# Settling keys and adding values one slot later, and pools whose tiles wait for their own bytes, in a two-layer Perceiver block on one core

## The chip, the core and the metric

The kernel runs on one core of a Trainium2 chip. The metric is the device time of one execution in microseconds. Of three runs the median is 1718.99 us (1718.89 to 1719.83). The core has five engines with a queue of instructions each: TensorE (PE in the profile; its weight loads are PEld), VectorE (DVE), ScalarE (ACT), GpSimd (POOL) and SyncE (SP, which here only issues loads and stores). They meet at semaphores.

## What is computed

x holds 512 tokens of width 512, the context 8192 rows of width 512. Two layers follow each other; a layer is three residual steps, each on a layer norm of x:

```
x = x + cross_attention(ln(x), context)   # 16 heads of 32; layer 0 also normalizes each head's q and k
x = x + self_attention(ln(x))             # layer 0: causal to later tokens; layer 1: a window of 64
x = x + experts(ln(x))                    # 8 experts, the best 2 of each token (silu / squared relu)
```

Cross attention is, per head, `softmax(q k^T masked) v`, with keys and values projected from the context. The masks leave few context rows in play (the inputs mask all but the tail), so the fast path looks for the tiles of 128 context rows that hold an unmasked row, up to 15 of them (SLOTS), and works on those alone. A path for more tiles is in the program and not run on these inputs.

## The kernel before

The order of stages is cross attention 0, self-attention 0, experts 0, cross attention 1, self-attention 1, experts 1. The framework (a tile scheduler) chooses the order of instructions on each engine when the program is built, mostly the order in which they are written, with a ready one put ahead of one that waits; it also adds the semaphores. Tiles come from pools. A pool is a stretch of SBUF (or of PSUM banks) and is opened and closed like a bracket, so that a later pool can take the memory of one that was closed. Within a pool a tag has a number of buffers, used in turn.

Cross attention (`attend_slots`) runs in two stages for each layer.

**The key stage** goes through the slots `s`. `keys(s)` projects a slot's keys into the one bank of `pacc`; in layer 0 VectorE adds the bias into a tile `kb` (L1051). `unit(s)` normalizes its heads (`unit_rows`: a square on ScalarE L1099, a sum L1101, a square root on ScalarE L172, a reciprocal L174, a product L1103). `settle(s)` transposes `kb` on TensorE (L1060, tile `ktp`) and ScalarE copies it with norm weights into `kT` (L1061). In layer 1 the keys are written into `kT` directly and `settle` and `unit` do nothing. `maxima(0, s)` makes the scores of the first of four groups of heads for that slot and takes running maxima on VectorE (`take`, L763 and L765). `values(s)` projects values (`pv`). In layer 0 `beside()` also goes through the second layer's mask: a load of 512 KB, a column on GpSimd and squares on ScalarE (L1204). The slot loop runs keys(s), settle(s-1), maxima(0, s-2), values in about half of the slots of layer 0, unit(s), beside. Ahead of it in layer 0 `queries` makes q in four token tiles with the same unit_rows; its tile `qb` shares the tag and two buffers with `kb`. Behind the loop come the last maxima, the row shifts of group 0 (`shift_of`: transposes `mtp`, then reductions) and the maxima of group 1 for four slots.

**The attention** goes through 4 groups x 15 slots. A step makes four score tiles (`sc`, four heads), subtracts the row maxima by a small matmul (L639), takes exponentials on ScalarE into a `pT` tile (L869), and adds the values of the step before (`accumulate`, tile `acc`, L824). The denominators are summed on GpSimd (VectorE in the last group) into `four` tiles (L842) and reduced by TensorE (L851); `divide` takes their reciprocal (L861). The first 41 steps also carry the maxima of a later group (`scm`), in two halves; the last 19 don't, and are called plain steps here. Work such as the outputs (`ops`, L712) is spread over later steps as fillers. PSUM has eight banks: four with tag `s`, three with `m`, one for `acc`; score tiles of plain steps take `s` and `m` in turn.

Self-attention and experts open their pools on memory that the stages before have used (`self_and_ffn`). The experts' layer norm writes `xn` (L189), transposes it (`lnt`, L192), makes router logits (`lps`, L1686), and only then knows which experts' weights to load (L1665, L1670). A branch (`tc.If`, for inputs with fuller experts) ends each expert stage and isn't taken.

Of the kernel before, what the change touches and what calls it, by code (L numbers as in the profile page):

```python
# [55 lines left out]
def tile_perceiver(  # L56
# [6 lines left out]

    const = ctx.enter_context(tc.tile_pool(name="const", bufs=1))
# [9 lines left out]
    dram = ctx.enter_context(tc.tile_pool(name="dram", bufs=1, space=bass.MemoryType.DRAM))  # L74
# [22 lines left out]
    with tc.tile_pool(name="begins", bufs=1) as tmp, tc.tile_pool(name="beginsps", bufs=1, space=PSUM) as tps:  # L97
        t = tmp.tile([1, NCHUNK, CH // P], F32, name="brow")
        nc.gpsimd.iota(
            t, pattern=[[NC * CH // P, NCHUNK], [1, CH // P]], base=0, channel_multiplier=0,  # L100
            allow_small_or_imprecise_dtypes=True,
        )
        tp = tps.tile([NKT, 1], F32, name="bcol")
        nc.tensor.transpose(tp, t.rearrange("p n i -> p (n i)"), ident[0:1, 0:1])
        nc.vector.tensor_copy(begins, tp)
# [311 lines left out]
    def cross_attention0():  # L417
        with ExitStack() as st:
            pool = st.enter_context(tc.tile_pool(name="c0", bufs=2))
            ctxp = st.enter_context(tc.tile_pool(name="ctxp0", bufs=2))  # L420
            psum = st.enter_context(tc.tile_pool(name="c0ps", bufs=2, space=PSUM))
            pacc = st.enter_context(tc.tile_pool(name="c0acc", bufs=1, space=PSUM))
# [3 lines left out]
            with tc.tile_pool(name="c0q", bufs=2) as qp:  # L426
# [8 lines left out]
            kvp = st.enter_context(tc.tile_pool(name="c0kv", bufs=NCHUNK // 2))  # L435
# [70 lines left out]
    def cross_attention1():  # L506
        with ExitStack() as st:
            pool = st.enter_context(tc.tile_pool(name="c1", bufs=2))
            ctxp = st.enter_context(tc.tile_pool(name="ctxp1", bufs=2))
            psum = st.enter_context(tc.tile_pool(name="c1ps", bufs=2, space=PSUM))  # L510
            pacc = st.enter_context(tc.tile_pool(name="c1acc", bufs=1, space=PSUM))
# [3 lines left out]
            with tc.tile_pool(name="c1q", bufs=2) as qp:  # L515
# [7 lines left out]
            kvp = st.enter_context(tc.tile_pool(name="c1kv", bufs=NCHUNK))  # L523
            mp = st.enter_context(tc.tile_pool(name="c1m", bufs=2))
# [212 lines left out]
    def attend_slots(pool, psum, pacc, kT, vN, qT, kbias, wo, bv, late, keys, settle, values, unit, more, early, aside, beside, extra):  # L737
# [47 lines left out]
        for s in range(n):  # L785
            keep(keys, s)
            if s >= 1:
                settle(s - 1)
            if s >= 2:
                maxima(0, s - 2)  # L790
# [5 lines left out]
            beside()  # L796
        settle(n - 1)
        steps = shift_of(0)
# [3 lines left out]
        keep(values, todo.pop(0))  # L802
# [11 lines left out]
        last = None  # L814

        def accumulate():

            if last is None:
                return
            g, i, pT = last  # L820
# [50 lines left out]
        for at in range(NG * n):  # L871
            g, i = divmod(at, n)
            mg, mi = divmod(at + n + LEAD, n)
            pT = late().tile([P, GH, S], F32, name="pT", tag="pT", bufs=4)
            if mg < NG:

                for j in range(2):
# [12 lines left out]
                    if j == 0:  # L890
                        accumulate()
# [3 lines left out]
            else:  # L895
# [7 lines left out]
                accumulate()  # L903
# [9 lines left out]
            last = (g, i, pT)  # L913
# [9 lines left out]
        accumulate()  # L923
        denominators(NG - 1, range(end - 2, end), end)
        for _, f in fillers:
# [30 lines left out]
    def cross_slots0():  # L956
        with ExitStack() as st:
            pool = st.enter_context(tc.tile_pool(name="f0", bufs=2))
            psum = st.enter_context(tc.tile_pool(name="f0ps", bufs=4, space=PSUM))
            pacc = st.enter_context(tc.tile_pool(name="f0acc", bufs=1, space=PSUM))  # L960
# [4 lines left out]
            kvp = kv.enter_context(tc.tile_pool(name="f0k", bufs=2))  # L965
            qp = kv.enter_context(tc.tile_pool(name="f0q", bufs=2))
# [57 lines left out]
            def queries(behind):  # L1024
                with tc.issue_after(behind.ins):
                    for t in range(NT):
# [6 lines left out]
                        qb = kvp.tile([P, D], F32, name="qb", tag="kb")  # L1033
# [13 lines left out]
            def keys(s):  # L1047
                pk = pacc.tile([P, D], F32, name="pk", tag="acc")
                half(s, 0, pk)
                kb = kvp.tile([P, D], F32, name="kb", tag="kb")  # L1050
# [32 lines left out]
            def late():  # L1083
                if not over:
                    kv.close()
                    over["pool"] = st.enter_context(tc.tile_pool(name="f0w", bufs=2))
# [18 lines left out]
    def cross_slots1(irow, kbias):  # L1105
        with ExitStack() as st:
            pool = st.enter_context(tc.tile_pool(name="f1", bufs=2))
            psum = st.enter_context(tc.tile_pool(name="f1ps", bufs=4, space=PSUM))
            pacc = st.enter_context(tc.tile_pool(name="f1acc", bufs=1, space=PSUM))
# [4 lines left out]
            kvp = kv.enter_context(tc.tile_pool(name="f1k", bufs=2))  # L1114
            qp = kv.enter_context(tc.tile_pool(name="f1q", bufs=2))
# [51 lines left out]
            def late():  # L1167
                if not over:
                    kv.close()
                    over["pool"] = st.enter_context(tc.tile_pool(name="f1w", bufs=2))  # L1170
# [87 lines left out]
    def self_attention0(pool):  # L1258
        with ExitStack() as st:
            psum = st.enter_context(tc.tile_pool(name="s0ps", bufs=3, space=PSUM))  # L1260
            pacc = st.enter_context(tc.tile_pool(name="s0acc", bufs=1, space=PSUM))
# [124 lines left out]
    def self_attention1(pool):  # L1386

        W = S + 2 * PAD
        with ExitStack() as st:
            psum = st.enter_context(tc.tile_pool(name="s1ps", bufs=3, space=PSUM))  # L1390
            pacc = st.enter_context(tc.tile_pool(name="s1acc", bufs=1, space=PSUM))
# [264 lines left out]
    def ffn(wp, pool, w1, w2, ff, layer, act, softmax_first, caps, order):  # L1656
# [20 lines left out]
        with ExitStack() as st:  # L1677
            psum = st.enter_context(tc.tile_pool(name="fps", bufs=2, space=PSUM))
            pacc = st.enter_context(tc.tile_pool(name="facc", bufs=1, space=PSUM))
            inner = st.enter_context(tc.tile_pool(name="finner", bufs=2))  # L1680
# [203 lines left out]
    def rest(wp, pool, weights, irow, place, gate, xn, n, act, caps):  # L1884

        with ExitStack() as st:
            psum = st.enter_context(tc.tile_pool(name="rps", bufs=2, space=PSUM))
            pacc = st.enter_context(tc.tile_pool(name="racc", bufs=1, space=PSUM))
# [256 lines left out]
```

## Time and profile before

| | |
|---|---|
| runs, median | 1718.99 us |
| profiled execution | 1715.68 us, its span 1713.8 us |
| mean granted TensorE clock | 0.941 |
| cross attention 0: head and key stage | 0 to 203 us |
| cross attention 0: attention, plain steps from 409 | 203 to 479 us |
| self-attention 0 | 479 to 650 us |
| experts 0 | 650 to 948 us |
| cross attention 1 (plain steps from 1299) | 954 to 1368 us |
| self-attention 1 | 1368 to 1493 us |
| experts 1 | 1493 to 1701 us |

The stretches are read from the order of instructions in time. In the page, "busy" is the time in which an engine had an instruction; a line of the slices has 40 digits, one for 42.8 us each, in tenths. A line of waits reads: the engine, tile and line that waited, the engine, tile and line that released it, then the total in us, how many times and the longest. A line of the timeline reads: start, length, engine, line, instruction, output and inputs, how many; in brackets the idle time ahead of it and who ended that.

### The profile page before, as it was taken

Reading aid. Unit: us, or ns where it says so; the run is one execution under the profiler, and the core shown is the slowest. Engines: PE = TensorE matmul, PEld = TensorE weight load, DVE = VectorE, ACT = ScalarE, POOL = GpSimd, SP = SyncE. Lnnn points to the kernel's source line nnn. Section 1 sums busy time; section 2 is a strip of 40 time slices with the busy share of each in tenths; the row PEclk is TensorE's granted clock in tenths of the full one; section 3 lists DMA queues with packets and bytes.
Section 4 is the critical chain, followed back from the end, with each engine's and each line's share of the span. In section 5 each row is a group of like instructions: output and inputs, shape, how many; then the busy total and the mean of one; then the engine's idle time right before and its main releaser. Section 6 shows DMA issues by size and latency. Waiting matters only on the chain. (4 is left out here: it accounts for less than half of the span.)

```text
span 1713.8 us, 24266 instructions
## 1 busy us (share of the span) xinstructions
PE 1566.6 (91%) x9933; PEld 914.2 (53%) x9933; DVE 775.0 (45%) x1394; ACT 569.5 (33%) x1079; POOL 424.9 (25%) x306
## 2 busy tenths in 40 slices
PE   3889999999979997999999799999999989679996
PEld 2333333333234446999999465433333245369995
DVE  5366677774633645111112233567765536831112
ACT  1366445556622132111111211165556612211110
POOL 4000057788110001000002100068776110010002
PEclk9999989999989977999999899999999989879997
DMA  7055200000030003878885400000000040064672
GB/s 247 24 161 178 74 1 1 1 1 1 1 129 1 1 1 134 311 265 286 282 295 171 155 25 19 25 1 1 1 1 1 1 151 10 15 224 171 219 265 90
DMA packets 87144, 168.79 MB, mean 98 GB/s; under 512 B 8450, under 2 KB 23842, under 8 KB 85600
## 3 DMA queue, kind: packets, MB, share of 16 engines
q1 hardware_dynamic: 78352, 147.87, 25.4%
q0 software_dynamic: 5440, 17.01, 2.8%
q10 hardware_dynamic: 3216, 2.11, 0.4%
q8 instruction: 84, 1.38, 0.3%
q14 instruction: 52, 0.43, 0.1%
HBM read 156.30 MB, written 9.63 MB: 97 GB/s over the span
## 5 line engine op out<-in xcount | busy, mean ns | idle before, releaser
L869 ACT ACTIVATE pT<-sc,kbias 128x512 f32<-128x512 f32 x480 | 299.1, 686 | 205.1 <-PE sc L639 142.4
L752 PE MATMUL sc<-qTf,kTf 32*128 32x512 f32 x1264 | 297.0, 653 | 6.4 <-DVE d L861 4.9
L765 DVE SCALAR_TENSOR_TENSOR mx<-scm,kbias,mx 128x512 f32<-128x512 f32 x312 | 215.4, 743 | 97.8 <-PE scm L752 95.5
L752 PE MATMUL scm<-qTf,kTf 32*128 32x512 f32 x656 | 240.8, 653 | 2.1 <-DVE mx L765 2.1
L1790 PE MATMUL y<-hT,w 128*128 128x160 f32 (+13 forms) x1536 | 212.3, 298 | 2.4 <-DVE hT L1965 2.3
L1790 PEld LDWEIGHTS y<-hT,w 128*128 128x128 f32 x1536 | 205.1, 197 | 4.4 <-DVE hT L1965 2.8
L1774 PE MATMUL hps<-tokens,w 128*128 128x160 f32 (+13 forms) x1536 | 207.0, 293 | 0.0
L1774 PEld LDWEIGHTS hps<-tokens,w 128*128 128x128 f32 x1536 | 198.7, 192 | 1.8
L842 POOL TENSOR_TENSOR four<-four,pT 128x2048 f32<-128x2048 f32 x42 | 190.6, 4538 | 9.7 <-ACT pT L869 6.7
L752 PEld LDWEIGHTS sc<-qTf,kTf 32*128 32x128 f32 x1264 | 90.6, 189 | 148.4 <-issue 111.9
L842 POOL TENSOR_TENSOR four<-pT 128x2048 f32<-128x2048 f32 x24 | 109.0, 4542 | 109.2 <-ACT pT L869 109.2
L824 PE MATMUL acc<-pT,vNf 128*32 128x512 f32 x960 | 133.8, 624 | 1.5 <-ACT o L831 1.5
L765 DVE SCALAR_TENSOR_TENSOR mx<-sc,kbias,mx 128x512 f32<-128x512 f32 x136 | 93.3, 744 | 79.8 <-PE sc L752 79.8
L1965 DVE TENSOR_TENSOR hT<-sg,hps 128x320 f32<-128x320 f32 (+7 forms) x64 | 27.9, 436 | 189.5 <-ACT sg L1964 189.5
L752 PEld LDWEIGHTS scm<-qTf,kTf 32*128 32x128 f32 x656 | 75.0, 188 | 49.8 <-DVE mx L765 38.0
L639 PE MATMUL sc<-shift,ones 3*128 3x512 bf16 (+3 forms) x544 | 100.2, 383 | 0.0
L1815 POOL DMA_DIRECT2D answers_d<-yb x17 | 9.4, 556 | 291.7 <-ACT yb L1808 291.7
L1964 ACT ACTIVATE sg<-hps 128x320 f32<-128x320 f32 (+7 forms) x64 | 25.3, 396 | 135.1 <-PE hps L1774 135.1
L1012 PE MATMUL pv<-wkvf,cslot 128*128 128x512 f32 x120 | 56.8, 617 | 13.3 <-DMA cslot<-in_ctxT 13.2
L824 PEld LDWEIGHTS acc<-pT,vNf 128*32 128x32 f32 x960 | 20.7, 109 | 87.7 <-issue 80.5
L653 DVE TENSOR_REDUCE neg<-mtp 128x4 f32<-128x512 f32 x64 | 41.2, 683 | 55.7 <-PE mtp L650 55.7
L1690 POOL DMA_DIRECT2D tokens_d<-xn x8 | 4.5, 569 | 241.3 <-issue 143.5
(331 smaller groups left out, 1844.5 us busy)
## 6 DMA issues: line engine op xcount, KB each, us to landing
w<-in_L_ffn_W SPq DMA_DIRECT2D x96, 1024.0 KB, 7.6
mi<-in_mask SPq DMA_DIRECT2D x32, 512.0 KB, 4.3
cslot<-in_ctxT SPq DMA_DIRECT2D x30, 256.0 KB, 4.3
answers_d<-yb POOLq DMA_DIRECT2D x15, 256.0 KB, 7.2
answers_d<-zero POOLq DMA_DIRECT2D x9, 256.0 KB, 3.2
wkvf<-in_L_xattn_WkvT ACTq DMA_DIRECT2D x4, 512.0 KB, 6.4
wq<-in_L_xattn_WqT SPq DMA_DIRECT2D x2, 1024.0 KB, 7.8
wof<-in_L_xattn_WoT SPq DMA_DIRECT2D x2, 1024.0 KB, 4.7
```

The lines of the kernel that those rows point to most:

```text
L639: nc.tensor.matmul(ps, lhsT=ones16[r, :], rhs=k.shifts[g][r, 0:w], start=start, stop=stop)
L653: nc.vector.tensor_reduce(neg[:, h, :], tp.rearrange("p (t k) -> p t k", k=P), AX.X, ALU.max, negate=True)
L752: nc.tensor.matmul(ps, lhsT=kT[HD * h : HD * (h + 1), g, i * P : (i + 1) * P], rhs=qT[HD * h : HD * (h + 1), g, :], start=True, stop=stop,)
L765: nc.vector.scalar_tensor_tensor(to, ps, b, to, ALU.add, ALU.max)
L824: nc.tensor.matmul(k.sums[g][HD * h : HD * (h + 1), :], lhsT=vN[:, i, g * P + HD * h : g * P + HD * (h + 1)], rhs=pT[:, h, :], start=(i == ...
L842: engine.tensor_tensor(to, parts[g][-1], pT, ALU.add)
L869: nc.scalar.activation(pT[:, h, :], ps, AF.Exp, bias=kbias[:, i : i + 1])
L1012: last = nc.tensor.matmul(ps.rearrange("p (g n) -> p g n", g=NG), lhsT=src[:, c, s % 2, :], rhs=wkv[:, :, c, i * P : (i + 1) * P], start=( ...
L1774: nc.tensor.matmul(ps[:, j, 0:k], lhsT=w1[:, c, f * P : (f + 1) * P], rhs=tokens[:, c, starts[r] : starts[r] + k], start=(c == 0), stop=(c ...
L1790: nc.tensor.matmul(accs[0][:, d, 0:k], lhsT=w2[:, f, d * P : (d + 1) * P], rhs=hT[:, f, 0:k], start=(c == 0 and f == 0 and d % 2 == 0), st ...
L1964: nc.scalar.activation(sg, ps, AF.Sigmoid)
L1965: nc.vector.tensor_tensor(dst, sg, ps, ALU.mult)
```

## The change

It has three parts.

1. In the key stage `settle` and `maxima` follow one slot later: keys(s), settle(s-2), maxima(0, s-3). Three maxima are left behind the loop, and the values that stood between the last maxima and the transposes stand between the maxima instead. `kb` and `qb` get three buffers.
2. In plain steps the values of two steps before are added (`accumulate(2)`) in place of those of the step before; the first 41 steps keep a lag of one. `pT` gets five buffers. Behind the last step the values are added in two calls, with the last denominators between.
3. Nearly all pools behind the constants are opened with `reuse_waits="tile"`. A tile of a pool on used memory then waits for the earlier users of its own bytes; without it, it waits until all of the overlapped pool is released.

```diff
+    def tile_pool(**kw):
+        return tc.tile_pool(reuse_waits="tile", **kw)
...
-            pool = st.enter_context(tc.tile_pool(name="f0", bufs=2))
+            pool = st.enter_context(tile_pool(name="f0", bufs=2))
...
         for s in range(n):
             keep(keys, s)
-            if s >= 1:
-                settle(s - 1)
             if s >= 2:
-                maxima(0, s - 2)
+                settle(s - 2)
+            if s >= 3:
+                maxima(0, s - 3)
...
+        settle(n - 2)
+        steps = shift_of(0)
+        maxima(0, n - 3)
+        keep(values, todo.pop(0))
         settle(n - 1)
-        steps = shift_of(0)
         maxima(0, n - 2)
         keep(values, todo.pop(0))
         maxima(0, n - 1)
-        keep(values, todo.pop(0))
         steps[0]()
         keep(values, todo.pop(0))
         steps[1]()
...
-        last = None
-        def accumulate():
-            if last is None:
+        behind = []
+        def accumulate(lag):
+            if len(behind) < lag:
                 return
-            g, i, pT = last
+            g, i, pT = behind.pop(0)
...
-            pT = late().tile([P, GH, S], F32, name="pT", tag="pT", bufs=4)
+            pT = late().tile([P, GH, S], F32, name="pT", tag="pT", bufs=5)
...
                     if j == 0:
-                        accumulate()
+                        accumulate(1)
...
                 for h in range(GH):
                     exp(pT, h, i, tiles[h])
-                accumulate()
+                accumulate(2)
...
-            last = (g, i, pT)
+            behind.append((g, i, pT))
...
-        accumulate()
+        accumulate(1)
         denominators(NG - 1, range(end - 2, end), end)
+        accumulate(1)
...
-                        qb = kvp.tile([P, D], F32, name="qb", tag="kb")
+                        qb = kvp.tile([P, D], F32, name="qb", tag="kb", bufs=3)
...
-                kb = kvp.tile([P, D], F32, name="kb", tag="kb")
+                kb = kvp.tile([P, D], F32, name="kb", tag="kb", bufs=3)
```

## The prediction

> **What bounds the kernel now.** I read the page first: which engine is full, and in which slices.
>
> ```profile
> PE 1566.6 (91%) x9933; PEld 914.2 (53%) x9933; DVE 775.0 (45%) x1394; ACT 569.5 (33%) x1079; POOL 424.9 (25%) x306
> ...
> PE   3889999999979997999999799999999989679996
> ...
> PEclk9999989999989977999999899999999989879997
> ```
>
> TensorE is busy 91% of the span and holds both expert stages and both steady attention stages at 9. So the change can win only where PE digits fall, about 147 us in all. I therefore asked who TensorE waits for, stage by stage. The layer 0 key stage (76 to 192 us), TensorE first and then ScalarE:
>
> ```profile
> PE ktp L1060 <- DVE kb L1103: 11.6, 7, 2.9
> PE pk L1012 <- DVE kb L1051: 1.7, 2, 1.4
> ```
>
> ```profile
> ACT un_v L172 <- DVE un_v L171: 29.8, 13, 3.2
> ```
>
> Seven times the transposes of a slot's keys (settle) stand waiting for the last step of that slot's normalization, which was begun one slot earlier. The head of the stage, where the queries are made (44 to 76 us):
>
> ```profile
> PE qtp L1038 <- DVE qb L1103: 4.9, 2, 3.8
> ```
>
> The plain steps of the attention (19 of 60 per layer, where no maxima of a later group are left), layer 0 at 409 to 479 us; layer 1 at 1299 to 1368 us gives the same two figures:
>
> ```profile
> PE sc L752 <- DVE d L861: 1.8, 1, 1.8
> PE acc L824 <- ACT o L831: 0.7, 1, 0.7
> ```
>
> The values matmul (acc) never waits long for an exponential here; ScalarE is the one that waits, 19.5 us for the scores. Granted clock beside some gaps (columns after the stretch: length, PE, PEld, DVE, ACT and POOL busy, clock, DMA):
>
> ```profile
> 66.00:70.00 4.00, 0.37 (x4) 0.40 (x5) 2.32 (x5) 0.84 (x2) 0.00 (x0) 1.00 0.00 0
> 70.00:74.00 4.00, 4.00 (x9) 1.70 (x8) 0.00 (x0) 0.78 (x1) 0.00 (x0) 0.58 0.00 0
> 90.00:94.00 4.00, 1.72 (x5) 0.42 (x3) 1.77 (x5) 3.21 (x8) 0.43 (x2) 1.00 0.57 146
> 94.00:98.00 4.00, 3.34 (x13) 1.51 (x14) 1.39 (x3) 3.85 (x11) 0.22 (x1) 0.57 0.73 234
> ```
>
> After a gap the next 4 us run at little more than half clock. Last, the handover from layer 0's self-attention to its experts, in order of time:
>
> ```profile
> 648.02 0.16 DVE L188 RECIPROCAL ln_r<-ln_r 128x1 f32<-128x1 f32 x1
> ...
> 650.24 0.69 DVE L715 TENSOR_TENSOR x<-x,ops 128x512 f32<-128x512 f32 x1 [1.28 <-PE ops L712]
> 650.84 1.00 DVE L189 TENSOR_SCALAR xn<-x,ln_m,ln_r 128x512 f32<-128x512 f32 x2
> ```
>
> The statistics of the first two token tiles are ready at 645.2 and 648.2, yet xn is written only after the last addition into x. xn is the first tile of a new pool, on memory of the attention's pool.
>
> **The change, step by step.**
>
> (a) *Settle two slots behind, layer 0.* A slot costs TensorE 3.4 us for keys, 0.5 for transposes, 1.0 for scores and in half of the slots 3.5 for values (starts in the timeline), 6.7 on average. The chain from the end of keys to the normalized row is 7.5 us (135.15 to 142.63, VectorE and ScalarE in turn). With one slot between, a slot without values covers too little of it; with two, 13.4 us cover it. All 11.6 us fall away, and the half-clock stretch behind the 2.9 us gap: 4 us at 0.57 lose 1.5 in work. Here I weigh a rule. The Trainium skill (TensorE: Matmul & The Clock Gate, "The HAM clock gate") says the clock falls after about 3.4 us of idling. By it the 2.9 us gap should have cost nothing more, and step (a) would be worth 11.6; the row shows 0.57 behind it, so 13.1. I take the row. A settle issues four transposes and one ScalarE copy (0.76 us), no DMA; the copy moves in ScalarE's queue ahead of the same squares as before. The mask's 30 loads of 512 KB must land in 103 us, 153 GB/s, where the expert stages take 280. What is late next: ScalarE is busy 74.4 us in these 116 and stands 29.8 us behind square roots whose input lies behind maxima on VectorE; that is 104, so the shorter stage (103) has no slack left there. The maxima themselves wait less for scores (15.2 us now) once settle doesn't hold them, so I give back 3 us, not 12. **-10**, from -3 (ScalarE holds it) to -13.
>
> Behind the loop one more set of maxima comes last, right ahead of the transposes of the maxima, without a values matmul between. Two takes at 0.74 must end first: 0 to +1.5 us per layer, by whether the last values go ahead of the transposes. The scores on VectorE behind that are its own bound (16 x 0.7), so I take 0. In layer 1 settle does nothing and the key stage is full (50.00 of 50 us): 0.
>
> (b) *A third kb buffer.* qb and kb share two. keys(0) ended at 53.3 but its addition waited until 76.03, behind qb of tile 3, for a buffer of a query tile that was still in work; meanwhile its only bank was held and TensorE had nothing for the 3.85 us at 65.8. keys(0) and values(4) filled the two gaps before. With three buffers that addition can stand at about 62.3, and keys(1), 3.4 us, fit into that gap. Full effect: 3.4, the half clock behind (4 us at 0.58: 1.7) and the 1.4 us wait of pk, 6.5. It rests on keys(1) being put there: **-3.5**, 0 to -6.5.
>
> (c) *Values two behind in the plain steps.* Here the lag could let TensorE run ahead of ScalarE. TensorE's own work in the stretch: 19 steps of 2.29 (scores 0.96, shift 0.33, values 1.0, spaced in the timeline), 43.5; transposes of maxima 2.0 and 0.3; denominators 3.6 + 2.0 + 0.9 + 0.9 + 1.9; outputs 3.8: 58.9 of 69.6 us. ScalarE needs 20 exponentials in 12.13 us, so 2.43 per step or 46. The skill's budget for one activation (ScalarE: Activation LUTs, "Rules for kernel authors": about 0.3 us and 0.83 ns per element, so by estimate 0.73, and 2.9 per step) speaks against the lag: ScalarE would be the bound in every bare step and 55 of the 69.6 us its own. The row, 2.43, puts the two engines level, so steps are lost on neither by much. Of the 10.7 us over TensorE's work, 6 (layer 1: 4.4) hang on a bank: the fourth score tile of one step waits until the reciprocals release the denominators' bank, and half clock follows. The lag doesn't touch this, unless values go ahead of the blocked score (up to 1 us and the clock loss). 0.7 is the copy of the finished accumulator; it slides along. Some 1.3 us are small waits on exponentials, which the lag removes mostly. At the end the last denominators precede the last values by 0.9 us, and the 1.76 us reciprocal behind them starts that much sooner. About 1.75 per layer, **-3.5**; +1 to -9. The fifth pT buffer holds a tile one step longer and hides under that.
>
> (d) *Pools whose tiles wait for their own bytes.* The loads issued early are mostly hidden anyway: behind layer 0's cross attention wq is issued at 487.16 and the projection at 495.57 waits for ScalarE's last xnT, not for a DMA. What counts is the tiles that engines write. At the self-attention to experts handover two token tiles can be normalized, transposed and routed before 650.84: from there TensorE does transposes 1.9, logits 3.6, and both again, 11 us until 662.46. With the first half gone into the 1.9 us gap at 647.2 and under the last tile's own chain, the rest ends near 658.5: **-3.5**, 0 to -6. At the experts to layer 1 handover the queue of loads waits for the branch (948.75 to 954.43); context tiles and wv may come before it, and a values matmul may fill part of the 8 us ahead of the first query projection (962.35): **-1.5**, 0 to -7. The other three handovers sit in VectorE's own chain of x, statistics, xn: **-1**, 0 to -5. On the queue of loads (SP) an early load that waits would hold the expert weights behind it; the last of these is issued at 911.35, and wq already waits alone until 948.10, so I count nothing. GpSimd's copies of narrow keys only come earlier. The steady stages have no such wait: 0.
>
> Sum: -10 - 3.5 - 3.5 - 3.5 - 1.5 - 1 = -23 us. The profiled execution took 1715.68 with a span of 1713.8; the span becomes 1690.8. The runs shown have a median of 1718.99, 3.3 above that execution, and I carry the offset: **1696**.
>
> **Rivals.**
>
> *The handovers give nothing, nor does the third buffer* (the waits belong to the chains, and order on the engines stays). For it: the layer norm chains named above. Against it: xn at 650.84. Left: -10 - 3.5, so 1705.5.
>
> *ScalarE takes back the key stage.* For it: 104 of 116 us already busy or blocked. (a) -3, the rest halved, -6.5: 1709.5.
>
> *More than I count*: keys(1) fill the gap, values fill the bank wait, work moves ahead of layer 1's projections. -13 - 6 - 6 - 5 - 5 - 2 = -37: 1682.
>
> *Slower.* One mechanism: ScalarE's square root. Per slot it works 5.0 us (74.4 over 15) and stands 2.0 (29.8 over 15) at the root. If the new order puts four takes (2.8 us) and a row's bias addition ahead of each variance, it stands 4. Then 15 slots take 15 x 9.0 = 135 instead of 116, +19; the remaining gains, -8 at best beside it, leave +11: 1730. It decides against the change from 15 x (5.0 + w) = 116 + 8, that is w = 3.3 us. Against it: no slot now exceeds 3.2, and the order of keys, maxima, norm inside a slot stays.
>
> *No change*: the freed waits return on neighbours one for one.
>
> **How the numbers follow.** Likeliest 0.48 (1696, own range 1689 to 1703); handovers and buffer nothing 0.17; ScalarE takes back 0.1; more 0.13; no change 0.06; slower 0.06. A measurement of this kernel tells about 0.2% from no change, 3.4 us: faster is below 1715.6. Faster: 0.48 + 0.17 + 0.1 + 0.13 = 0.88, less 0.03 for the last of the ScalarE case ending above 1715.6: 0.85; same 0.08, slower 0.07. Range: below 1681 only half of "more" is left out; above 1713 lie slower, no change and a little of the ScalarE case. 1681 to 1713.
>
> **What would show it.** (a) right: no line "ktp waits for kb" above 2 us, the stage from 76 us about 103 long, granted clock near 1.00 throughout; wrong: the same total on un_v, pk or square. (b): pk between two qps, no 0.58 stretch near 70. (c): plain stretches of 67 to 68 us, reciprocal d still ahead of sc; wrong if it is gone. (d): xn of the first token tiles ahead of the last addition into x; context loads ahead of the branch. The prediction is wrong on the whole if orders on an engine change in the expert stages or the steady attention, which I hold at zero.

## The result, and the profile after

The changed kernel takes 1706.21 us (median of 4 runs, 1703.6 to 1708.57) where the kernel before takes 1718.94: a ratio of 0.9926, 95% interval 0.9906 to 0.9946. It is 12.7 us faster. The forecast was 23 us, so the direction and the range held and the size did not. The profiled execution took 1708.26 us with a span of 1706.4. That is only 7.4 us less than the profiled execution of the kernel before (1715.68), so what the stages below show adds up to 7.4 and not to 12.7.

The page of the changed kernel, the same rows as before:

```profile
PE 1566.9 (92%) x9933; PEld 914.2 (54%) x9933; DVE 773.4 (45%) x1394; ACT 568.5 (33%) x1079; POOL 424.5 (25%) x306
...
PE   3899899999979997999999899999999989679996
...
PEclk9999889999999987999999899999999989879996
```

TensorE's busy time is unchanged (1566.6 before), so between these two executions the gain is idle time. (Time at half clock counts as busy.) The waits of TensorE, VectorE and ScalarE in the key stage of layer 0 (76 to 192 us):

```profile
DVE un_s L1108 <- ACT un_q L1106: 29.8, 14, 3.0
ACT un_v L176 <- DVE un_v L175: 27.9, 12, 2.8
...
PE pk L1019 <- DVE kb L1058: 5.1, 5, 1.4
DVE mx L769 <- PE sc L756: 4.8, 3, 3.6
PE pv L1019 <- ACT vNf L1028: 3.5, 2, 2.4
```

The line "ktp waits for kb", 11.6 us before, is gone. In its place the next keys wait for the addition that empties their bank (1.7 before, 5.1 now), and the values for a copy by ScalarE (3.5). Higher up stands what makes these late: VectorE waits 29.8 us for the squares `un_q` of ScalarE, against this line of the kernel before:

```profile
DVE un_s L1101 <- ACT un_q L1099: 9.7, 11, 2.4
```

One slot of the new chain in VectorE's timeline shows how a wait for ScalarE reaches TensorE:

```profile
126.59 0.69 DVE L1108 TENSOR_REDUCE un_s<-un_q 128x16 f32<-128x512 f32 x1 [2.24 <-ACT un_q L1106]
127.20 2.06 DVE L769 SCALAR_TENSOR_TENSOR mx<-sc,kbias,mx 128x512 f32<-128x512 f32 x3
129.17 0.17 DVE L175 TENSOR_SCALAR un_v<-un_s 128x16 f32<-128x16 f32 x1
129.62 0.25 DVE L178 RECIPROCAL un_r<-un_v 128x16 f32<-128x16 f32 x1 [0.28 <-ACT un_v L176]
129.91 0.69 DVE L1110 TENSOR_TENSOR kb<-kb,un_r 128x512 f32<-128x512 f32 x1
130.52 0.68 DVE L1058 TENSOR_TENSOR kb<-pk,bkf 128x512 f32<-128x512 f32 x1
```

The keys had ended at 128.7. Their addition, the last line, stands on VectorE behind the whole normalization of the slot before, and the following keys could start at 131.26 only. What the first line waited for is to be seen on ScalarE:

```profile
121.87 0.22 ACT L176 ACTIVATE un_v<-un_v 128x16 f32<-128x16 f32 x1 [2.81 <-DVE un_v L175]
121.99 0.70 ACT L1211 ACTIVATE square<-mi,first 128x512 f32<-128x512 int32 x1
...
124.56 0.72 ACT L1211 ACTIVATE square<-mi,first 128x512 f32<-128x512 int32 x1
...
125.28 0.76 ACT L1068 ACTIVATE kTf<-ktp,norms 128x512 f32<-128x512 f32 x1
125.94 0.62 ACT L1106 ACTIVATE un_q<-kb 128x512 f32<-128x512 f32 x1
```

The keys of this slot were in `kb` at 123.7 (their addition on VectorE, 123.01 and 0.68 long), but four squares of the mask and the copy into `kT` stood ahead of un_q. The squares in turn had stood behind the square root of the slot before, for which ScalarE was idle 2.81 us, because three maxima (2.06 us) lie on VectorE between the sum and the variance. So in most slots each of the two engines waits once for the other.

TensorE's waits in the head of that stage (44 to 76 us), and in the plain steps (405 to 475 us):

```profile
PE qtp L1045 <- DVE qb L1110: 4.9, 2, 3.8
```

```profile
PE sc L756 <- DVE d L867: 1.8, 1, 1.8
PE acc L830 <- ACT o L837: 0.8, 1, 0.8
```

These are as before. The clock beside the gaps (66 to 74 and 90 to 98 us):

```profile
66.00:70.00 4.00, 0.48 (x5) 0.51 (x6) 2.21 (x5) 0.84 (x2) 0.00 (x0) 1.00 0.00 0
70.00:74.00 4.00, 4.00 (x8) 1.71 (x7) 0.00 (x0) 0.78 (x1) 0.00 (x0) 0.59 0.00 0
90.00:94.00 4.00, 4.00 (x14) 1.70 (x14) 3.12 (x7) 3.84 (x12) 0.29 (x2) 1.00 0.62 150
94.00:98.00 4.00, 4.00 (x11) 1.67 (x10) 1.53 (x4) 2.67 (x8) 0.37 (x2) 1.00 1.01 344
```

The gap at 90 us and the half clock behind it went with the settle wait. The gap near 66 and its 0.59 stayed. Last, VectorE at the handover to the experts:

```profile
644.31 0.15 DVE L192 RECIPROCAL ln_r<-ln_r 128x1 f32<-128x1 f32 x1
...
646.52 0.69 DVE L719 TENSOR_TENSOR x<-x,ops 128x512 f32<-128x512 f32 x1 [1.28 <-PE ops L716]
647.12 1.00 DVE L193 TENSOR_SCALAR xn<-x,ln_m,ln_r 128x512 f32<-128x512 f32 x2
```

xn still comes right behind the last addition into x.

To compare stages I use stretches between instructions that all kernels have, and beside each length the time that the clock took from it: length times one minus the mean granted clock. "Key stage" runs from the end of the queries' last transposes to the end of the transposes of maxima (the expectations below count it from the second keys, which makes it 4.1 us longer). All are layer 0 unless marked, one profiled execution each.

| kernel | key stage | clock took | plain steps | clock took | outputs to next projection, L1 | experts 0 to layer 1's queries |
|---|---|---|---|---|---|---|
| before | 123.0 | 1.2 | 69.4 | 3.5 | 19.4 | 14.3 |
| changed | 120.2 | 1.2 | 68.8 | 3.4 | 16.7 | 11.9 |
| part 1 alone | 120.6 | 0.0 | 66.4 | 0.0 | 18.8 | 14.2 |
| part 2 alone | 123.9 | 1.2 | 65.6 | 0.0 | 17.2 | 14.3 |
| part 3 alone | 125.8 | 3.8 | 68.0 | 2.0 | 19.5 | 11.8 |

Every run, profiled or not, has a span and a mean granted clock. The same split over whole spans, averaged over the runs of a kernel, doesn't rest on one execution (standard errors: 0.5 to 1.4 us for what the clock took, 0.2 to 0.9 for what is left):

| kernel | runs | mean clock | clock took | what is left of the span |
|---|---|---|---|---|
| before | 64 | 0.938 | 107.1 | 1608.7 |
| changed | 4 | 0.942 | 98.9 | 1605.4 |
| part 1 alone | 22 | 0.941 | 101.4 | 1606.8 |
| part 2 alone | 22 | 0.940 | 103.0 | 1609.1 |
| part 3 alone | 22 | 0.940 | 102.9 | 1608.7 |
| before, scan moved | 6 | 0.940 | 101.6 | 1601.8 |
| changed, scan moved | 5 | 0.943 | 95.6 | 1593.1 |

A low clock costs nothing while TensorE stands, so "clock took" is an upper bound. Still it says that much of what the change gained is clock: of 11.5 us of mean span, up to 8.2 are the clock's share and 3.3 are the rest. (The last two kernels come under "The scan elsewhere".)

### The profile page after: what moved, and what is told of

The parts are those of the page before. It is cut to its first block, busy times and chain, and to the rows that moved or that the text cites. A ratio compares the mean times of both kernels' runs of the same rounds, so it can differ in the third digit from the quotient of the medians.

```text
span 1706.4 us, 24173 instructions
## 1 busy us (share of the span) xinstructions
PE 1566.9 (92%) x9933; PEld 914.2 (54%) x9933; DVE 773.4 (45%) x1394; ACT 568.5 (33%) x1079; POOL 424.5 (25%) x306
## 5 line engine op out<-in xcount | busy, mean ns | idle before, releaser
L756 PE MATMUL sc<-qTf,kTf 32*128 32x512 f32 x1264 | 302.4, 657 | 6.1 <-DVE d L867 4.7
L848 POOL TENSOR_TENSOR four<-four,pT 128x2048 f32<-128x2048 f32 x42 | 190.6, 4539 | 11.5 <-ACT pT L875 8.6
L1972 DVE TENSOR_TENSOR hT<-sg,hps 128x320 f32<-128x320 f32 (+7 forms) x64 | 27.9, 437 | 189.7 <-ACT sg L1971 189.7
L1019 PE MATMUL pv<-wkvf,cslot 128*128 128x512 f32 x120 | 58.3, 631 | 16.0 <-DMA cslot<-in_ctxT 12.5
```

What stands on the lines that cost most here:

```text
L756: nc.tensor.matmul(ps, lhsT=kT[HD * h : HD * (h + 1), g, i * P : (i + 1) * P], rhs=qT[HD * h : HD * (h + 1), g, :], start=True, stop=stop,)
L848: engine.tensor_tensor(to, parts[g][-1], pT, ALU.add)
L1019: last = nc.tensor.matmul(ps.rearrange("p (g n) -> p g n", g=NG), lhsT=src[:, c, s % 2, :], rhs=wkv[:, :, c, i * P : (i + 1) * P], start=( ...
```

## The experiments

Four theories for the missing gain of the key stage go through the expectations. T1: the loads of the mask's pieces wait for ScalarE's squares of earlier pieces, by their three buffers. T2: ScalarE's own queue of squares sets the pace. T3: VectorE's chain of one slot after another sets it. T4: the one bank of keys does.

**Each part alone.** Three kernels, each the kernel before with one of the three parts of the change. Of each part's edit one line stands here, parts 1, 2 and 3 in turn:

```diff
-                settle(s - 1)
+                settle(s - 2)
...
-                accumulate()
+                accumulate(2)
...
-            pool = st.enter_context(tc.tile_pool(name="f0", bufs=2))
+            pool = st.enter_context(tile_pool(name="f0", bufs=2))
```

> Part 1 of the change alone on the kernel before: keys settle two slots behind, the last maxima ahead of the last values, three kb buffers. By the prediction's own terms (a) -10 and (b) -3.5: the time 13.5 us under the kernel before, the stage from the second keys to the last transposes of maxima of layer 0 at about 114. By what the trace of the changed kernel suggests, that another pace takes the place of the settle wait (two slots stay near 15 us): the stage near 124 instead of 127.1, the time about 3 us under the kernel before (2 to 5). The line of transposes waiting for kb is gone by both.

> Part 2 alone on the kernel before: values two slots behind in plain steps, five pT buffers. By the prediction's term (c): -3.5 us. By the landmarks of the changed kernel (plain steps of layer 0 0.6 shorter, of layer 1 0.8 longer, the end of layer 1 2.1 shorter): between 0 and -2. If the values now wait on a bank elsewhere, up to +1.

> Part 3 alone on the kernel before: pools whose tiles wait for their own bytes. By the prediction's term (d): -6 us, of which 3.5 between self-attention and experts of layer 0, and 1.5 between experts and layer 1. By the landmarks of the changed kernel: 0.4 at the first, 2.4 at the second, of which the head of layer 1 gives up to 2.8 back, and some 2 at the last handover: -1 to -5 in all. If layer 1's head gives back because its first projections come at a lower clock, the same must show here, with no part of the settle change in the kernel.

Measured, as ratios to the kernel before (22 runs each): part 1 0.9955 (0.9943 to 0.9968), part 2 0.9981 (0.9965 to 0.9997), part 3 0.9981 (0.9964 to 0.9998). Times 1717.6 that is -7.7 us (-9.8 to -5.5), -3.3 (-6.0 to -0.5) and -3.3 (-6.2 to -0.3), -14.3 together: within their intervals the parts add up to the whole. Part 1 lies between the two expectations. Its key stage is only 2.4 shorter in the profile; the profiled execution gained 3.0 and 1.5 more in the plain steps of the two layers, which part 1 does not touch, because there the clock did not fall. Part 3 gains 2.5 ahead of layer 1's queries and, in this profile, nothing else beyond the clock's share. Its layer 1 key stage is 146.8 us, as before: the changed kernel's 150.2 is not a price of the pools. It is the clock's: parts 1 and 2 alone show 148.3 and 149.3 there, and without what the clock took (0 to 3.0 us) all five kernels have 146.3 to 147.2.

**More buffers for the mask's pieces.**

```diff
-            mi = pool.tile([P, n, S], I32, name="mi8", tag="mi8", bufs=3)
+            mi = pool.tile([P, n, S], I32, name="mi8", tag="mi8", bufs=5)
```

> The changed kernel with five buffers in place of three for the pieces of layer 1's mask that are scanned beside layer 0's key stage. Theory T1, the load of a piece waits for ScalarE's squares of the piece three earlier and so paces the slots: the key stage shrinks from 124 to 114 to 118 us, the wait of squares for the first word (7.4 us) falls, the time falls by 6 to 10 us. Theory T2, ScalarE's own work and order (58 us of squares among 76 busy) paces it: stage and time within 1 us of the changed kernel. Theory T3, the chain of additions, square root and multiplication between VectorE and ScalarE paces it through the one bank of keys: also within 1 us.

Measured: 0.9936 (0.9917 to 0.9955), where the changed kernel has 0.9926. The profiled key stage is 118.3, 1.9 shorter, and none of it is to be seen in the times. ScalarE's wait for the column that GpSimd makes of a piece, 7.4 us, fell to 5.4 only. The 6 to 10 us of T1 are out.

**Half of the squares.** ScalarE squares each piece of the second layer's mask in two halves; one is left out, so that half of this work on the mask is not done. (The sums that are then not written are set to zero once.) All loads stay as they are.

```diff
-            for j in range(n):
+            for j in range(1):
```

> The changed kernel with one of the two squares for each piece of the mask left out: half of the mask's row check is not computed, some 29 us of ScalarE's work in layer 0's key stage go. Theory T2, ScalarE's own queue of squares holds each slot's chain: the stage from the second keys to the last transposes of maxima goes from 124 to 112 to 116, the time 8 to 11 us under the changed kernel. Theory T3, VectorE takes the slots' chains one after the other (addition, sum of squares, three maxima, square root, reciprocal, multiplication, next addition): the squares only lengthen it by the time that the sum waits for ScalarE's un_q, 29.8 us in the changed kernel; about half of that goes, of which less than half reaches TensorE: 3 to 6 us.

Measured: 0.986 (0.9839 to 0.9881), 11.3 us under the changed kernel, some 5 to either side. The key stage is 110.4, which is 114.5 as the expectation counts. This is T2's size; T3 had 3 to 6. Nor can it be the loads of the mask, which are all still there. In the same window VectorE and TensorE now show:

```profile
DVE un_s L1108 <- ACT un_q L1106: 10.8, 12, 2.4
```

```profile
PE pv L1019 <- ACT vNf L1028: 1.5, 1, 1.5
PE pk L1019 <- DVE kb L1058: 1.4, 1, 1.4
```

The wait for un_q falls by 19 us, and TensorE's two new waits fall from 8.6 to 2.9 with it.

**The order on VectorE.** The normalization of a slot is written one slot later.

```diff
-            unit(s)
+            if s >= 1:
+                unit(s - 1)
...
+        unit(n - 1)
```

> The changed kernel with one line moved: the normalization of a slot's keys is written one slot later, behind the addition of the next slot's keys, so that on VectorE the addition that frees the bank of keys no longer stands behind the previous slot's square root. No engine's work changes, the mask's squares stay. Theory T3: TensorE no longer waits for the bank (5.1 us) and little for the copies of values: the stage goes from 124 to 113 to 117, the time 6 to 10 us under the changed kernel. Theory T2, ScalarE's work in order sets the pace whatever VectorE's order is: under 2 us.

Measured: 0.9938 (0.9917 to 0.9959), no gain, a key stage of 121.1 and a wait for un_q of 29.5 us. The run decides less than it was meant to. The framework puts an instruction that is ready ahead of one that waits, and in the steady part of the stage VectorE's order came out as before: product of the slot before, addition, one of the maxima, sum, the others, square root, reciprocal. The addition never came to stand in front: ScalarE's un_q still waits for the addition of its own slot (at 122.71, 0.98 us) and the sum follows it. T3 is decided further down, by a kernel in which that order is the same and the squares are gone.

**A second bank for keys.**

```diff
-                pk = pacc.tile([P, D], F32, name="pk", tag="acc")
+                if s % 2:
+                    pk = psum.tile([P, D], F32, name="pk", tag="m", bufs=3)
+                else:
+                    pk = pacc.tile([P, D], F32, name="pk", tag="acc")
```

> The changed kernel with keys of odd slots in a second bank of PSUM, one of those of the values. If the one bank of keys is itself the cause (theory T4): the waits of keys for the addition go (5.1 us), the time 4 to 6 us under the changed kernel. Theory T3, the chain through VectorE has its own period of 7.5 us per slot: TensorE runs one set of keys ahead and then waits elsewhere as long, at most 2 us, of which some from the head, where keys can start earlier.

Measured: 0.9893 (0.9869 to 0.9917), 5.7 us under the changed kernel, which is T4's size, but with an interval of about 5 us on that difference and not by T4's way. In the key stage TensorE still waits:

```profile
PE pv L1019 <- DVE kb L1061: 6.1, 5, 2.3
PE pv L1019 <- ACT vNf L1028: 2.8, 2, 2.6
PE pk L1019 <- ACT vNf L1028: 1.7, 2, 1.6
```

The waits for a bank moved from the keys to the values, which share theirs. What is gained is the head: the timeline has keys at 57.4, 67.3 and 73.8 us, between the queries, where the changed kernel has a gap of 3.85 us and half clock. By the edit these are slots of the second bank, the second and the fourth: the third slot's bank holds the first keys until their addition at 74.58.

**Keys ahead of the queries.**

```diff
-                        qb = kvp.tile([P, D], F32, name="qb", tag="kb", bufs=3)
+                        qb = kvp.tile([P, D], F32, name="qb", tag="qb", bufs=2)
...
+            keys(0)
+            queries(valued)
```

> The changed kernel with the first slot's keys written ahead of the queries, and queries and keys in buffers of their own (2 and 3). The prediction's step (b) said that a third buffer frees the first addition of keys, which still comes at 75.9 us, behind the addition of the last query on VectorE. If order on VectorE and not the buffer held it: the addition comes before 60 us, the next keys fill the gap of 3.85 us near 66 and the half clock behind it goes: 3.5 to 6.5 us less, unless the key stage takes it back. If a buffer is what holds it, nothing changes by this edit that the third buffer did not change: within 1 us.

Measured: 0.991 (0.9889 to 0.9932), 2.7 us under the changed kernel and not told from it. VectorE's first addition of keys comes at 50.34 us instead of 75.92, which a third shared buffer had not done. The next keys do start in the gaps (53.6, 64.3 and 69.9 us), but a new wait of 3.54 us appears ahead of the last transposes of queries (at 84.00), and the clock takes 4.5 us of the key stage instead of 1.2. The profile puts the wait down to a square of the mask; the query rows that these transposes read were ready at 83.85 only. No run separates the two.

**The scan elsewhere.** All of the mask's scan is moved into layer 0's self-attention, one piece after every second item of its order; in the changed kernel and, the same edit, in the kernel before.

```diff
-                more, EARLY, aside, scanned, [listing] * 6,
+                more, EARLY, aside, lambda: None, [],
...
+            def scanned():
+                count[0] += 1
+                if count[0] % 2 == 0 and scan.i < 32:
+                    scan.step(pool)
...
```

> The changed kernel with the scan of layer 1's mask moved from layer 0's key stage into layer 0's self-attention, where ScalarE is busy 38 of 150 us. All work is still done. If ScalarE's squares hold the key stage (theory T2): the stage at 111 to 115 us instead of 124, the time 9 to 13 us under the changed kernel, 1693 to 1697. If self-attention pays for the squares (a row of exponentials behind two squares, 1.8 us each, 30 times at worst): the gain is gone.

> The kernel before with the same move of the mask's scan and nothing of the change. It tells what settling two slots behind is worth once ScalarE is free. The three parts together are 12.7 us with the squares in place, and parts 2 and 3 alone are 3.3 each. If the squares took the lag's gain (T2): this kernel keeps its wait of transposes for kb (8 to 12 us), gains 2 to 6 us against the kernel before, and the changed kernel with the same move is 16 to 21 below it. If the lag is worth little by itself: this kernel gains as much from the move as the changed one (9 to 13), and the difference stays 12 to 13.

Measured: 0.9845 (0.9822 to 0.9868), 1690.56 us, on the changed kernel, 13.9 under it, some 5 to either side; 0.9927 (0.9905 to 0.9949), 1705.9, on the kernel before. The key stages of the two, TensorE's waits in the kernel with the change first:

```profile
PE pk L1020 <- DVE kb L1059: 1.4, 1, 1.4
PE mtp L654 <- DVE mx L770: 0.9, 1, 0.9
```

```profile
PE ktp L1061 <- DVE kb L1104: 8.1, 7, 1.2
PE pk L1013 <- DVE kb L1052: 1.7, 2, 1.4
```

and VectorE in the first of them:

```profile
DVE un_s L1109 <- ACT un_q L1107: 1.2, 2, 1.1
```

VectorE's order in the steady part is that of the changed kernel, and still nothing waits. So its chain does not hold the pace by itself (T3); it hands on what ScalarE is late by: 29.8 us of waiting for un_q with all squares, 10.8 with half, 1.2 with none. With ScalarE free the lag does what it was forecast to do: the stage is 108.8 us with the change and 116.7 without, 7.9 apart where it was 2.8 apart with the squares in place. The totals of the medians are less clear than the stages: the two kernels differ by 14.1 us, 5.5 to either side, which excludes neither 16 to 21 nor 12 to 13. And the kernel before gained 12.5 us (9 to 16) from the move, where 2 to 6 were expected if the squares had taken the lag's gain. Two things explain it in part. Some 7 us of the gain of both kernels lie behind the key stage (205.4 to 198 up to the plain steps, 2 to 4 of them clock), where the listing of the mask's rows had been spread; in the key stage alone the move is worth 6.3 to the kernel before and 11.4 to the changed one. And the clock's share also fell. Without that share, over all runs, the kernels with and without the change are 3.3 us apart with the squares in place and 8.7 with them moved (standard error 1 for each), which bears the stages out.

Self-attention 0 pays nothing for the squares (155.0 us against 155.5), though ScalarE is busy there 86 us instead of 38. But the handover to the experts is 2.4 us longer with the change and 3.4 without (32.1 and 33.1 against 29.7): the last steps of the listing now stand on VectorE between the last addition into x and xn.

**The denominators' bank.** The prediction left a wait of 1.8 us in the plain steps as out of reach of the change. Here ScalarE copies the sums out of their bank, and the reciprocals read the copy.

```diff
+            if g < NG - 1:
+                dens[g, 0] = late().tile([P, S], F32, name="d", tag="d", bufs=1)
+                nc.scalar.copy(dens[g, 0], dens[g])
...
-            nc.vector.reciprocal(dens[g, 0][:, r], dens[g][:, r])
+            nc.vector.reciprocal(dens[g, 0][:, r], dens[g, 0][:, r])
```

> The changed kernel with the sums of the exponentials copied from their bank by ScalarE (0.65 us, where it stands 3.6 us) and the two reciprocals, 1.76 us each, made from the copy. The prediction left the wait of the fourth score tile for that bank (1.8 us per layer, followed by 4 to 8 us at 0.52 to 0.64 of the clock in most executions) as untouched by step (c). If the wait and the clock behind it are what the plain steps lose: 1.8 per layer and 1.7 to 3.4 for the clock, 5 to 9 us in all under the changed kernel, plain steps of 63.5 to 65.5 us instead of 68.8. If only the wait goes: 3.5. If ScalarE or the order of exponentials takes it back: 0 to 1.

Measured: 0.9942 (0.9925 to 0.9958), no gain. Yet the plain steps came out as expected: 63.6 us in both layers at full clock, 5.2 less. The loss is where the same division falls into paired steps. TensorE at one of these:

```profile
304.62 0.71 PE L756 MATMUL scm<-qTf,kTf 32*128 32x512 f32 x1 [1.34 <-DVE mx L769]
...
305.15 1.03 PE L756 MATMUL scm<-qTf,kTf 32*128 32x512 f32 x1
```

The changed kernel waits 0.26 us at that place. Here it is 1.34, for maxima that stand behind the reciprocals on VectorE, and the matmuls behind it take 1.03 instead of 0.59. From the maxima to the plain steps the stage is 213.5 us, of which the clock took 19.2, against 204.6 and 10.2.

**A version from these findings.** The changed kernel with the scan moved, the second bank of keys, and the copy of the sums for the third group alone, whose division falls into the plain steps:

```diff
+            if g == NG - 2:
+                dens[g, 0] = late().tile([P, S], F32, name="d", tag="d", bufs=1)
+                nc.scalar.copy(dens[g, 0], dens[g])
+                dens[g] = dens[g, 0]
...
-            if i == 0:
+            if i == 0 and g < NG - 2:
```

> The changed kernel with three edits that the earlier runs pointed to: the mask's scan in layer 0's self-attention, keys of odd slots in a second bank, and the copy of the sums by ScalarE for the group alone whose division falls into the plain steps (copied for all groups, it put a wait of 1.34 us for maxima and half clock behind the division into two paired steps of each layer). From the kernel with the scan moved alone (1690.6): plain steps of 63.6 instead of 67.2 and 67.5 us, 3.6 to 3.9 per layer; no new wait in the paired steps; keys of the second slot in the gap ahead of the last queries, 3 to 5. In all 1679 to 1683. If the banks of keys and values crowd each other once ScalarE is free: 1683 to 1686.

Measured: 1678.91 us, 0.9781 (0.9752 to 0.981), some 38 us under the kernel before (43 to 33). Plain steps take 63.6 us in both layers, no wait of 1.34 is left in the paired steps, and in the key stage TensorE waits for little:

```profile
PE pv L1024 <- DVE kb L1066: 1.3, 5, 0.3
PE mtp L654 <- DVE mx L770: 0.9, 1, 0.9
PE pk L1024 <- DVE kb L1066: 0.2, 1, 0.2
```

## Why the prediction was right or wrong

**Step (a), settling two slots behind, forecast -10: the mechanism right, the price given back far too small.** The 11.6 us wait and the half clock at 94 us went. The stage became 2.8 us shorter in the profile. The failed term is "I give back 3 us": it summed ScalarE's busy time and its waits for the variance (104 of 116 us) and concluded that a stage of 103 just fits. In the changed kernel the same sum over the same 116 us is 75.7 and 27.9, again 104: ScalarE had not come free any sooner. A sum of busy time doesn't say what stands ahead of what. Squares of the mask, 0.9 us each with the read of their sum, stand on ScalarE ahead of un_q; VectorE stands still until un_q comes (29.8 us instead of 9.7), and behind it on VectorE stands the addition that empties the bank of keys. Taking half of the squares away gave 11.3 us, moving all of them (and the listing) 13.9, and then the lag itself was worth 7.9 of the forecast 10 in the key stage. The rival "ScalarE takes back the key stage", with -3 for (a), was this one; it was given a tenth. The sign of being wrong that the prediction named, the same total on un_v (27.9 after 29.8), came too. The buffers of the mask and VectorE's chain by itself were tested as other causes and fell. One thing was not tried: to put the maxima on VectorE behind the variance, which would shorten ScalarE's idle time with the squares in place.

Part 1 alone measured -7.7, though, 2.9 beyond the difference of the two profiled executions (-4.8). The table of all runs says what the rest is: the clock took 101.4 us instead of 107.1, and what is left fell by 1.9 only. The profiled execution of the kernel before, at 0.941, had lost less to the clock than its runs did on average (0.938), so its profile shows too little of it. In which stages the other executions lose it the runs don't show; that the seven waits of up to 2.9 us in the old order are among them is argued, not shown.

**Step (b), the third buffer, forecast -3.5: wrong, 0.** "Behind qb of tile 3, for a buffer" was an inference from a place in the timeline. The trace of the kernel before already spoke against it:

```profile
69.63 0.63 PE L1038 MATMUL qtp<-ident,qb 128*128 128x128 f32 x4 [3.85 <-DVE qb L1103]
```

```profile
75.42 0.69 DVE L1034 TENSOR_TENSOR qb<-qps,bc_L_xattn_bq 128x512 f32<-128x512 f32 x1 [5.94 <-PE qps L1029]
76.03 0.68 DVE L1051 TENSOR_TENSOR kb<-pk,bkf 128x512 f32<-128x512 f32 x1
```

With two buffers in turn, the first keys take that of the third query, and its transposes ended at 70.3. VectorE then stood idle for the last query until 75.42, with the addition of keys in its queue behind. With three buffers the addition stayed at 75.92 us, right behind that of the last query, while the transposes that free the second query's buffer end at 62. It moved to 50.34 when the call was written ahead of the queries. That run also gave queries and keys buffers of their own, so it does not split the two by itself; with these rows it is order, not memory. The gap is real and worth about what was said: keys in it are most of what the second bank gained.

**Step (c), values two behind, forecast -3.5: size right (-3.3 alone) by luck, places wrong in the main.** Without what the clock took, the plain steps of layer 0 went from 65.9 to 65.4 and those of layer 1 from 66.0 to 65.4: about 0.5 each, not 1.75. The earlier reciprocal at the end did not come either: the values of the last step but one fill the place, and from the start of the last exponentials to that reciprocal it is 5.40 us before and 5.43 after. What came instead is the clock: over all runs of part 2 alone it took 103.0 us instead of 107.1, and what is left of the span did not fall (1609.1 after 1608.7). Part of it has a place. The last values now lie in the wait of the outputs, which shrinks from 2.87 to 2.09 and 2.34 us. Of the 8 such places in the four kernels without part 2, 5 took more than 18.5 us up to the next projection; of the 20 in the ten kernels with it, 2, the others mostly 16.5 to 17.2. At some 2.5 us each this is, by estimate, 2 to 3 us for both layers. The bank wait stayed, as said, and was worth more than (c): 5.2 us per layer when it was taken away.

**Step (d), the pools, forecast -6: half, -3.3 alone.** Ahead of layer 1's queries -1.5 was forecast and 2.4 to 2.5 came, in both kernels with part 3. The mechanism was not quite the one named: context loads still come behind the branch, but wq is issued at 930.57 instead of 948.10, and layer 1's first transposes wait 7.4 us for xn where they waited 10.1. VectorE's first instruction behind the branch, in the kernel before and in the changed one:

```profile
954.43 1.29 DVE L182 BATCH_NORM_STATS2 ln_s<-x 128x6 f32<-128x512 f32 x2 [5.68 <-SPq L1881]
```

```profile
946.50 1.29 DVE L186 BATCH_NORM_STATS2 ln_s<-x 128x6 f32<-128x512 f32 x2 [3.04 <-DVEq L1888]
```

L1881 is the branch, and SPq is the queue of loads. Before, that queue held wq until the last matmul of the experts (a wait of 9.2 us for xps) and came to the branch late; the profile puts VectorE's wait down to it. The wait is 5.5 to 5.7 us in all four kernels without part 3 and 3.0 to 3.1 in all ten with it. So the part did act by letting a load go early, which the prediction had called "mostly hidden anyway", and not by tiles that engines write. At the self-attention to experts handover -3.5 was forecast and 0 came (29.7 us from the last outputs to the first expert matmul, before and after). The failed reading is "xn is the first tile of a new pool, on memory of the attention's pool": that was true, and not why it was late. Freed from the pool's release, xn stayed behind the last addition into x. Whether its own bytes or the written order hold it there was not tried. The other three handovers gave nothing that the stretches show, against -1.

Of the stages held at zero, attention 0 up to the plain steps and experts 0 are 0.8 and 1.6 us shorter in the profiles, attention 1 is 1.6 shorter, and layer 1's key stage 3.4 longer, of which the clock took 3.0. Misses (a) and (b) share a reading: a wait was put down to distance or to memory where a place in an engine's queue held it; at the handover of (d) that is likely and not shown. That the measured time still came within the range is in part luck: in the table of all runs up to 8.2 of 11.5 us are clock, of which the steps had named some 3.

## What to carry to other kernels

When a wait is removed by a longer lag, follow the chain that fed it as a loop through the engines' queues, place by place: lag hides a chain's length, not its period, and side work ahead of one small instruction can set that period while its engine is far from full (here ScalarE, busy 76 of 116 us). In these traces a gap on TensorE costs its length and, often, half the clock for 4 to 8 us behind it, so price short gaps by both, and compare stages, and runs, with the clock's share taken out. Before a late instruction is blamed on a buffer, look when that buffer came free, and what stood ahead of the instruction on its own engine.

## What the hardware showed that was not expected

The same short gap is followed by half clock in one execution and not in the next. Two kernels at the wait of 1.8 us in the plain steps, the 4 us ahead of its end and 8 us behind it (columns: stretch, length, PE, PEld, DVE, ACT and POOL busy, clock, DMA); the kernel before, then part 1 alone, which has the same instructions there:

```profile
435.10:439.10 4.00, 2.22 (x22) 0.53 (x18) 4.00 (x4) 2.42 (x4) 0.04 (x1) 1.00 0.00 0
439.10:443.10 4.00, 4.00 (x14) 0.61 (x14) 1.96 (x1) 2.12 (x4) 3.90 (x2) 0.52 0.00 0
443.10:447.10 4.00, 4.00 (x28) 1.18 (x28) 0.00 (x0) 1.65 (x4) 0.75 (x1) 0.63 0.00 0
```

```profile
433.40:437.40 4.00, 2.26 (x18) 0.46 (x14) 4.00 (x4) 2.42 (x4) 0.00 (x0) 1.00 0.00 0
437.40:441.40 4.00, 3.96 (x30) 1.19 (x34) 2.04 (x1) 2.71 (x5) 3.86 (x2) 1.00 0.00 0
441.40:445.40 4.00, 4.00 (x30) 1.20 (x23) 1.76 (x1) 4.00 (x8) 0.83 (x1) 1.00 0.00 0
```

In the twelve kernels with this wait, 1.74 to 1.81 us long in each of two layers, the clock fell (0.72 or less in the next 4 us) in 19 cases of 24 and cost 2.0 or 3.4 to 3.5 us where it fell. The Trainium skill (TensorE: Matmul & The Clock Gate, "The HAM clock gate") has the clock fall after one idle window of about 3.4 us and says that the window runs freely, so that the number of slow matmuls at a kernel's start varies between runs. Here the fall behind a gap varies in the same way; that a whole window must be idle is not seen, since 1.8 us were enough in most cases. One profile therefore could not place gains of 2 or 3 us: the kernel before ran from 1710.52 us, at a mean clock of 0.942, to 1725.83, at 0.931, over 64 runs.
